# Expert remainders in quarters of 32 slots instead of whole tiles of 128

## The chip, the cores and the metric

The kernel runs on one core of one Trainium2 chip. The metric is the device time of a run in microseconds. The engines are named as the profile names them: PE (TensorE matmul), PEld (its weight load), DVE (VectorE), ACT (ScalarE), POOL (GpSimd) and SP (SyncE, which here issues DMAs).

## The reference

The computation is one gated cross-attention block followed by a mixture of experts, all in float32. There are 8 batches of 256 tokens (2048 tokens, width 256), a context of 120 rows for each batch, 16 heads of 64, and 8 experts with a hidden width of 1024, of which each token uses two.

```python
x = x + tanh(g_xattn[0]) * xattn(layernorm(x), ctx, w_q, w_kv, w_out, b_out)

def ffn(x):                                  # of layernorm(x) again
    probs = softmax(x @ Wr.T)                # 8 experts
    topk_vals, topk_idx = top_k(probs, 2)
    gate = topk_vals / topk_vals.sum(-1)     # placed at the two experts
    h = silu(einsum('btd,efd->btef', x, W1))
    y = einsum('btef,edf->bted', h, W2)
    return einsum('bte,bted->btd', gate, y)

x = x + tanh(g_ffn[0]) * ffn(layernorm(x))
```

The reference computes every expert for every token and weights most of them by zero. The kernel computes only the two chosen experts of each token, so there are 4096 pairs of a token and an expert, here called slots.

## The kernel before, in words

**Attention, 0 to some 272 us.** A loop over 32 units (8 batches, 2 halves of the heads, 2 halves of the tokens) computes projections, scores, softmax and the output projection. Behind it the router picks two experts for each token (`router`), and `places` sends each token's row, with its eight gates and its token number, into a list in memory, `routed`, once for each chosen expert. Each expert has its own stretch of 2048 rows in that list. Rows that no token was sent to stay filled with zeros and a token number past the end, so they add nothing to the output.

**Expert stage, from some 272 us.** The work is done in tiles of 128 slots of one expert. A tile is loaded from the list (`load`), turned so that its 256 columns lie on partitions (`turn`: two PE transposes and a DVE copy), multiplied by W1 (`up`: 16 matmuls of 128 columns and the silu on ACT), multiplied by W2 (`down`: 8 matmuls of 256 columns), scaled by its gates on DVE, and added to its tokens' rows in memory by an indirect add on POOL. The adds wait for one another, one at a time, because two of them may name the same token.

Three kinds of tile follow one another. Eight "first" tiles hold the first 128 slots of each expert; they can start before the router has seen all tokens. Eight "last" tiles hold each expert's last, part-empty 128 slots; their expert is known when the program is built, so their weights are read where they lie, in `w_sb`. The "full" tiles are the whole tiles between; which expert they belong to is known only on the chip, so their place and expert are read from a table (`table`, small DVE operations, built once after tile 4), and DVE first copies the expert's W1 and W2 (2048 elements a partition each, L688 and L697) into fixed buffers. With the full tiles numbered 0 to 28 from the back, 9 to 28 always run, and 0 to 8 are inside a conditional block (L933) that runs only if there are more than 20.

**Order of the work.** PE, DVE, ACT and SP run in the order in which the program is written; POOL's order is the scheduler's. The loop at L930 is software-pipelined: step i does the up of tile i, opens tile i+1 (its weights, its turn), and then does the down of tile i-1. `load` runs four tiles ahead on SP. Up to and including full tile 12 the sums go into a buffer `acc` in memory; then SP copies `acc` to the output (L764) and the last 16 tiles add into the output directly. SP's later loads stand behind that copy in its queue.

Of the kernel before, what the change touches and what calls it, by code (L numbers as in the profile page):

```python
# [33 lines left out]

EARLY = 2
FULLS = 29
SURE = 16
SPARE = 9
# [6 lines left out]
def tile_gated_xattn_moe(  # L45
# [19 lines left out]
    late = ctx.enter_context(tc.tile_pool(name="late", bufs=1))  # L65
# [58 lines left out]
    nc.gpsimd.iota(number, [[P, NBLK]], base=0, channel_multiplier=1)  # L124
    empty = w_sb[:, 2, :XW]
# [453 lines left out]


    def row(tag, n, dtype=F32):
        return small.tile([P, n], dtype, tag=tag, name=tag, bufs=1)

    def table():


        tiles_i = row("tiles_i", E, I32)
        nc.vector.scalar_tensor_tensor(
            tiles_i, count(NBLK, fw[2]), -1.0, bump, ALU.add, ALU.add
        )  # L590
        nc.vector.tensor_scalar(tiles_i, tiles_i, 7, None, ALU.arith_shift_right)
        full = row("full", E)
        nc.vector.tensor_scalar(full, tiles_i, -1.0, 0.0, ALU.add, ALU.max)
        second = row("second", E)
        nc.vector.tensor_scalar(second, first_row, float(P), None, ALU.add)
        last_row = row("last_row", E, I32)
        nc.vector.scalar_tensor_tensor(
            last_row, full, float(P), second, ALU.mult, ALU.add
        )
        upto = row("upto", E)  # L600
        one8 = row("one8", E)
        nc.vector.memset(one8, 1.0)
        nc.vector.tensor_tensor_scan(upto, one8, full, 0.0, ALU.mult, ALU.add)
        total_i = row("total_i", 1, I32)
        nc.vector.tensor_copy(total_i, upto[:, E - 1 : E])

        at = row("at", FULLS)
        nc.gpsimd.iota(
            at, [[1, FULLS]], base=-FULLS, channel_multiplier=0,
            allow_small_or_imprecise_dtypes=True,  # L610
        )
        nc.vector.tensor_scalar(at, at, upto[:, E - 1 : E], None, ALU.add)
        past = fp.tile([P, FULLS, E], F32, tag="y", name="past")
        skipped = fp.tile([P, FULLS, E], F32, tag="y", name="skipped")
        shape = [P, FULLS, E]
        nc.vector.tensor_tensor(
            past,
            upto.unsqueeze(1).to_broadcast(shape),
            at.unsqueeze(2).to_broadcast(shape),
            ALU.is_le,  # L620
        )
        nc.vector.tensor_tensor(
            skipped, past, full.unsqueeze(1).to_broadcast(shape), ALU.mult
        )
        expert = row("expert", FULLS)
        nc.vector.tensor_reduce(expert, past, AX.X, ALU.add)
        expert_i = row("expert_i", FULLS, I32)
        nc.vector.tensor_copy(expert_i, expert)
        before_it = row("before_it", FULLS)
        nc.vector.tensor_reduce(before_it, skipped, AX.X, ALU.add)  # L630
        nc.vector.tensor_tensor(before_it, at, before_it, ALU.subtract)
        nc.vector.tensor_scalar(before_it, before_it, float(P), None, ALU.mult)
        nc.vector.scalar_tensor_tensor(
            expert, expert, float(T), before_it, ALU.mult, ALU.add
        )
        used = row("used", FULLS)
        nc.vector.tensor_scalar(used, at, 0.0, None, ALU.is_ge)
        nc.vector.tensor_scalar(expert, expert, float(P - NOWHERE), None, ALU.add)
        nc.vector.tensor_tensor(expert, expert, used, ALU.mult)
        full_row = row("full_row", FULLS, I32)  # L640
        nc.vector.tensor_scalar(full_row, expert, float(NOWHERE), None, ALU.add)
        return last_row, expert_i, full_row, total_i
# [5 lines left out]
    def take(pool, shape, tag, name, **kw):  # L648
        if spare is None:
            return pool.tile(shape, F32, tag=tag, name=name, **kw)  # L650
        if tag not in spare:
            spare[tag] = pool.tile(shape, F32, tag=tag, name=name, **kw)
        return spare[tag]


    def load(t):
        kind, i = t
        xt = take(fp, [P, XW], "xt", f"xt_{kind}{i}", bufs=6)
        if kind == "first":
            first = nc.sync.dma_start(xt, routed[ds(i * T, P), :])  # L660
            for send in behind:
                tc.declare_no_dep(
                    first.ins, send.ins, reason="rows behind those of the first tiles"
                )
            firsts.append(first)
            return xt
        last_row, _, full_row, _ = tables[0]
        if kind == "last":
            start = nc.sync.value_load(
                last_row[0:1, i : i + 1], min_val=0, max_val=NOWHERE - P  # L670
            )
        else:
            start = nc.sync.value_load(
                full_row[0:1, i : i + 1], min_val=0, max_val=NOWHERE
            )
        nc.sync.dma_start(xt, routed[ds(start, P), :])
        return xt

    def weights(t, xt):

        kind, i = t
        if kind != "full":
            w2 = part(i, DC * DFF, FC, D)
            return part(i, 0, DC, DFF), xt[:, D + i : D + i + 1], lambda: w2
        expert_i = tables[0][1]
        e = nc.vector.value_load(expert_i[0:1, i : i + 1], min_val=0, max_val=E - 1)
        w1 = take(fw[0], [P, DC, DFF], "w1", f"w1_{i}")
        nc.vector.tensor_copy(  # L688
            w1.rearrange("p c f -> p (c f)"),
            w_sb[:, ds(e, 1), : DC * DFF].rearrange("p e f -> p (e f)"),  # L690
        )
        gate = take(fp, [P, 1], "gate", f"gate_{i}", bufs=4)
        nc.vector.tensor_copy(gate, xt[:, D : D + E][:, ds(e, 1)])

        def copy_w2():
            w2 = take(fw[0], [P, FC, D], "w2", f"w2_{i}")
            nc.vector.tensor_copy(  # L697
                w2.rearrange("p c d -> p (c d)"),
                w_sb[:, ds(e, 1), DC * DFF :].rearrange("p e f -> p (e f)"),
            )  # L700
            return w2

        return w1, gate, copy_w2
# [9 lines left out]
    def up(t, xT, w1):  # L713
# [10 lines left out]
        hT = take(fp, [P, FC, P], "hT", f"hT_{t[0]}{t[1]}")  # L724
# [5 lines left out]
    def down(t, hT, gate, xt, w2):  # L730
        py = take(fw[2], [P, 512], "mm", f"py_{t[0]}{t[1]}")
        for f in range(FC):
# [7 lines left out]
        y = take(fp, [P, D], "y", f"y_{t[0]}{t[1]}")  # L740
        nc.vector.tensor_scalar(y, py[:, :D], gate, None, ALU.mult)  # L741
        sure = t[0] == "full" and t[1] >= FULLS - SURE
        add = nc.gpsimd.indirect_dma_start(  # L743
            out=out[:, :] if sure else acc[:, :],
            out_offset=bass.IndirectOffsetOnAxis(
                ap=xt[:, XID : XID + 1].bitcast(I32), axis=0
            ),
            in_=y,
            in_offset=None,
            compute_op=ALU.add,  # L750
        )

        if last_add:
            tc.add_manual_dep(
                add.ins,
                last_add[-1].ins.name,
                mybir.DependencyInfo(
                    mybir.DependencyClass.Sync, mybir.DependencyReason.DATA
                ),
                reason="sums of one token",  # L760
            )
        last_add.append(add)
# [4 lines left out]

    fw = []
    state = {"ready": None, "pending": None}
# [15 lines left out]
    order += [("last", e) for e in range(E)]  # L785
    order += [("full", j) for j in range(SPARE, FULLS)]
    AHEAD = 4
# [130 lines left out]

    for name, kw in (
        ("fw", {}),  # L920
        ("ps_ph", {"space": bass.MemoryType.PSUM}),
        ("ps_py", {"space": bass.MemoryType.PSUM}),
    ):
        fw.append(
            ctx.enter_context(tc.tile_pool(name=name, bufs=2, reuse_waits="tile", **kw))
        )
# [3 lines left out]
    for i, t in enumerate(order):  # L930
        if i == 16:

            with tc.If(total > FULLS - SPARE):  # L933
                spare = {}
                for j in range(SPARE):
# [4 lines left out]
                    down(tj, up(tj, turn(tj, xt), w1), gate, xt, w2)  # L940
                spare = None
        if i == 12:
            total_i = tables[0][3]
            total = nc.values_load(total_i[0:1, 0:1], min_val=0, max_val=FULLS)
        w2_of = state["ready"][2][2]
        if i == 2:
            turn_y(B - 1, bank_tr)
        new = go_up()
        copies = []
# [9 lines left out]
        if i + 1 < len(order):  # L959
            open_tile(order[i + 1], xts[i + 1])  # L960
        if i == 0:
# [9 lines left out]
        state["pending"] = *new, w2  # L971
        if i == 1:
# [10 lines left out]
        if i == 4:  # L983
            tables.append(table())
        while len(xts) <= min(i + AHEAD, len(order) - 1 if tables else 7):
            xts[len(xts)] = load(order[len(xts)])
        if i == 1:
# [46 lines left out]
```

## Time and profile before

| | |
|---|---|
| Time, median of 3 runs | 560.39 us (560.38 to 560.48) |
| The profiled execution's own time | 560.78 us |
| Its span | 559.0 us |
| TensorE clock granted in the span | 0.995 |
| PE busy | 545.2 us, 98% |
| DVE, ACT, POOL busy | 267.5, 192.3, 117.9 us |
| PE idle between 331 and 397 us | 0.0 us |
| PE idle between 397 and 551 us | 2.2 us |

A row of the profile gives the line, the engine, the operation, what is written and read with the shapes, how often, the busy time and the mean duration of one, and then the idle time of the engine just before those instructions with what ended it. Matmuls are pipelined, so the durations of neighbours overlap; the step from one start to the next tells what one costs. The rows in order of time begin with the start and the duration in microseconds.

### The profile page before, as it was taken

To read this page: it belongs to the slowest core of one execution; us is meant where nothing else is said; L and a number is where in the kernel's file an instruction comes from. 1 tells how busy PE (TensorE), PEld (TensorE's weight loads), DVE (VectorE), ACT (ScalarE), POOL (GpSimd) and SP (SyncE) were. 2 spreads that over 40 slices of the span, in tenths; PEclk is the share of its full clock that TensorE was granted. 3 is DMA by queue.
4 is the path that set the end of the run, shared out by engine and by line. 5 is a ranking of instruction groups with operands and counts; after the bars stand their busy time and mean duration, and the time that the engine had idled before them with its cause. 6 is when DMAs were issued, how large, how long until landed. Compare 5 with 4: busy or idle time off the path is not lost. (4 is left out here: it accounts for less than half of the span.)

```text
span 559.0 us, 9985 instructions
## 1 busy us (share of the span) xinstructions
PE 545.2 (98%) x3830; PEld 475.4 (85%) x3830; DVE 267.5 (48%) x612; ACT 192.3 (34%) x669; POOL 117.9 (21%) x129
## 2 busy tenths in 40 slices
PE   8999999999999999999999999999999999999992
PEld 7788878878788787887788999999999999999992
DVE  2666565568665686545743431111344444444430
ACT  1676464664655546556501211111111111111110
POOL 1021100101341013200035442222222132112222
PEclk9999999999999999999999999999999999999998
DMA  8999980500515001120499432222222522222111
GB/s 294 335 315 300 292 225 1 170 21 25 204 41 171 20 21 39 40 59 1 168 351 336 121 88 38 39 31 38 42 38 34 167 55 44 40 38 39 20 20 19
DMA packets 47586, 60.65 MB, mean 108 GB/s; under 512 B 3088, under 2 KB 42640, under 8 KB 47504
## 3 DMA queue, kind: packets, MB, share of 16 engines
q1 hardware_dynamic: 40400, 50.26, 29.3%
q0 software_dynamic: 6720, 9.06, 9.4%
q10 hardware_dynamic: 416, 0.66, 0.4%
q8 instruction: 32, 0.52, 0.4%
q14 instruction: 18, 0.15, 0.1%
HBM read 31.17 MB, written 30.89 MB: 111 GB/s over the span
## 5 line engine op out<-in xcount | busy, mean ns | idle before, releaser
L505 ACT ACTIVATE pr<-psc,mx 128x120 f32<-128x120 f32 x256 | 88.2, 370 | 64.2 <-DVE mx L499 64.2
L717 PEld LDWEIGHTS ph_full<-xT_full,w 128*128 128x128 f32 x640 | 74.5, 192 | 1.6 <-issue 0.7
L717 PE MATMUL ph_full<-xT_full,w 128*128 128x128 f32 x640 | 74.8, 276 | 0.3 <-PEq L933 0.3
L733 PE MATMUL py_full<-w,hT_full 128*128 128x256 f32 x320 | 72.2, 380 | 0.0
L733 PEld LDWEIGHTS py_full<-w,hT_full 128*128 128x128 f32 x320 | 59.4, 190 | 7.2
L725 ACT ACTIVATE hT_full<-ph_full 128x1024 f32<-128x1024 f32 x20 | 20.5, 1024 | 125.0 <-PE ph_full L717 125.0
L455 PE MATMUL pq<-xnT,w_sb 128*128 128x256 f32 x256 | 62.7, 389 | 0.4 <-DVE xnT L174 0.4
L549 PE MATMUL pw<-w_sb 128*128 128x256 f32 x256 | 58.6, 383 | 0.0
L455 PEld LDWEIGHTS pq<-xnT,w_sb 128*128 128x128 f32 x256 | 46.7, 190 | 10.7 <-issue 3.1
L505 ACT ACTIVATION_READ_ACCUMULATOR pr<-psc,mx 128x1 f32 x256 | 55.4, 216 | 0.0
L549 PEld LDWEIGHTS pw<-w_sb 128*128 128x128 f32 x256 | 47.5, 190 | 8.7 <-issue 2.5
L493 DVE TENSOR_REDUCE mx<-psc 128x8 f32<-128x960 f32 x32 | 37.0, 1157 | 37.0 <-PE psc L485 36.8
L743 POOL DMA_INDIRECT out_dram<-y_full,xt_full x16 | 26.5, 1658 | 86.5 <-DVE y_full L741 69.4
L332 POOL DMA_INDIRECT routed<-rows,slot x32 | 31.7, 992 | 56.4 <-DVE slot L328 49.4
L525 ACT COPY w_sb<-tr 120x512 f32<-120x512 f32 x64 | 34.6, 596 | 19.4 <-PE tr L524 19.4
L514 DVE TENSOR_TENSOR pr<-pr,sm 128x960 f32<-128x960 f32 x32 | 37.0, 1158 | 1.1
L485 PE MATMUL psc<-kT,w_sb 64*128 64x120 f32 x512 | 37.2, 284 | 0.0
L485 PEld LDWEIGHTS psc<-kT,w_sb 64*128 64x128 f32 x512 | 31.2, 187 | 6.4 <-issue 3.4
L524 PEld LDWEIGHTS tr<-ident,pr 128*120 128x120 f32 x256 | 29.5, 138 | 5.9 <-issue 4.3
L524 PE MATMUL tr<-ident,pr 128*120 128x128 f32 x256 | 33.5, 273 | 0.1
L440 PEld LDWEIGHTS pk<-ctxT_sb,w_sb 128*128 128x128 f32 x256 | 30.9, 192 | 0.8
L534 PE MATMUL po<-w_sb 120*64 120x256 f32 x256 | 31.3, 386 | 0.0
(138 smaller groups left out, 697.3 us busy)
## 6 DMA issues: line engine op xcount, KB each, us to landing
routed<-w_sb SPq DMA_DIRECT2D x8, 2120.0 KB, 22.3
w_sb<-in_w1T_dram SPq DMA_DIRECT2D x8, 1024.0 KB, 5.4
w_sb<-in_w2T_dram SPq DMA_DIRECT2D x8, 1024.0 KB, 10.3
xt_full<-routed SPq DMA_DIRECT2D x20, 132.5 KB, 2.1
acc<-x SPq DMA_DIRECT2D x8, 256.0 KB, 2.4
x<-in_x_dram SPq DMA_DIRECT2D x7, 256.0 KB, 2.8
w_sb<-in_w_kv_dram SPq DMA_DIRECT2D x3, 512.0 KB, 8.6
xt_first<-routed SPq DMA_DIRECT2D x8, 132.5 KB, 2.9
```

What stands on the lines that cost most here:

```text
L332: send = nc.gpsimd.indirect_dma_start(out=routed[:, :], out_offset=bass.IndirectOffsetOnAxis(ap=slot[:, i : i + 1], axis=0), in_=rows[h][: ...
L455: nc.tensor.matmul(pq[:, i, :], lhsT=wq_sb[:, c, ts(2 * h + i, P)], rhs=xnT[:, c, :], start=(c == 0), stop=(c == DC - 1),)
L485: nc.tensor.matmul(psc[:, j, ts(i, M)], lhsT=qT[ts(j, DH), 4 * o + i, ts(nb, P)], rhs=kT[ts(j, DH), 4 * o + i, :], start=True, stop=True,)
L493: nc.vector.tensor_reduce(mx.rearrange("p (j i) -> p j i", i=4), psc[:, :, : 4 * M].rearrange("p j (i m) -> p j i m", m=M), AX.X, ALU.max,)
L505: nc.scalar.activation(pr[:, h, :], psc[:, j, ts(i, M)], AF.Exp, bias=mx[:, h : h + 1], scale=QK_SCALE, accum_out=sm[:, h : h + 1],)
L514: nc.vector.tensor_tensor(pr, pr, sm.unsqueeze(2).to_broadcast([P, 8, M]), ALU.mult)
L524: nc.tensor.transpose(tr[:M, i, :], pr[:, 4 * j + i, :], ident)
L525: nc.scalar.copy(pT_sb[:, ts(j, 4), ts(nb, P)], tr[:M, :, :])
L534: nc.tensor.matmul(po[ts(j, DH), k, :], lhsT=v_sb[b % 2][:, ts(2 * (4 * o + i) + j, DH)], rhs=pT_sb[:, 4 * j + i, :], start=True, stop=True,)
L549: nc.tensor.matmul(pw[:, :D], lhsT=oT_sb[b % 2][:, ci, ts(k, P)], rhs=wo_sb[:, ci, :], start=(ci == 0), stop=(ci == IC - 1),)
L717: nc.tensor.matmul(ph[:, f, :], lhsT=w1[:, c, ts(f, P)], rhs=xT[:, c, :], start=(c == 0), stop=(c == DC - 1),)
L733: nc.tensor.matmul(py[:, :D], lhsT=hT[:, f, :], rhs=w2[:, f, :], start=(f == 0), stop=(f == FC - 1),)
```

## The change

The eight last tiles go. What remains of each expert behind its whole tiles is handled in one of two ways: a remainder of more than 96 slots is still a whole tile (now one of the full tiles, with its weights copied by DVE), and a smaller one is split into quarters of 32 slots. Four quarters, of any experts, make one tile, a "quad". The full tiles are now numbered 0 to 30 and 8 to 30 always run; two quads always run, and full tiles 0 to 7 and quads 2 to 5 are in the conditional block.

A quad is loaded by an indirect gather on POOL. For each quarter, ACT copies the expert's weights into a shared buffer (`fill`), half of the hidden width at a time. The matmuls of a quarter write 32 partitions, each quarter its own. With a half of the hidden width at a time the steps are: fill W1, turn, up, silu and fill W2, transposes of the hidden rows, down. These twelve steps are put between the steps of four whole tiles, tiles 8 to 11 for the first quad and 12 to 15 for the second, in each tile three of them. Each quad ends with four indirect adds of 32 rows, one for each quarter, because one token may be in two quarters.

The table is built in two parts, after tiles 4 and 5. The copy of `acc` to the output comes after full tile 15 instead of 12.

```diff
-FULLS = 29
-SURE = 16
-SPARE = 9
+QUARTER = 32
+FULLS = 31
+SURE = 15
+SPARE = 8
+QUADS = 6
+MIXED = 2
...
     number = const.tile([P, NBLK], I32, name="number")
     nc.gpsimd.iota(number, [[P, NBLK]], base=0, channel_multiplier=1)
+    places_w = const.tile([P, FULLS], F32, name="places_w")
...
+    nc.vector.tensor_scalar(
+        quarter_i, number[:, 0:1], 5, None, ALU.arith_shift_right
+    )
+    lane = const.tile([P, 1], F32, name="lane")
...
+    for q in range(QUADS):
+        nc.vector.tensor_scalar(
+            places_q[:, q : q + 1], quarter_i, float(4 * q), None, ALU.add
+        )
...
+    def sought(tag, at, upto, count, begin, step):
...
+        past = fw[0].tile(shape, F32, tag="w1", name=f"past_{tag}")
+        nc.vector.tensor_tensor(
+            past,
+            upto.unsqueeze(1).to_broadcast(shape),
+            at.unsqueeze(2).to_broadcast(shape),
+            ALU.is_le,
+        )
...
     def table():
...
+        nc.vector.tensor_scalar(tails, left, float(P - QUARTER), None, ALU.is_gt)
...
+        which, first = sought("w", at, upto, counts, begin, P)
...
+        yield expert_i, full_row
+
+        quarters = row("quarters", E)
+        nc.vector.tensor_scalar(quarters, left, 0.0, None, ALU.is_gt)
+        for k in range(1, 3):
+            nc.vector.scalar_tensor_tensor(
+                quarters, left, float(k * QUARTER), quarters, ALU.is_gt, ALU.add
+            )
...
+        which, first = sought("q", places_q, upto_q, quarters, begin[:, :E], QUARTER)
...
+        nc.vector.tensor_tensor(more_i, more, more_q, ALU.add)
+        yield quad_row, own, experts_i, more_i
...
     def load(t):
...
-        if kind == "last":
-            start = nc.sync.value_load(
-                last_row[0:1, i : i + 1], min_val=0, max_val=NOWHERE - P
-            )
+        if kind == "quad":
+            nc.gpsimd.indirect_dma_start(
+                out=xt,
+                out_offset=None,
+                in_=routed[:, :],
+                in_offset=bass.IndirectOffsetOnAxis(
+                    ap=tables[1][0][:, i : i + 1], axis=0
+                ),
+            )
+            return xt
...
+    def add_up(t, y, xt, parts=1):
...
+        for k in range(parts):
+            own = ts(k, P // parts)
+            add = nc.gpsimd.indirect_dma_start(
+                out=out[:, :] if sure else acc[:, :],
+                out_offset=bass.IndirectOffsetOnAxis(
+                    ap=slots[:, k : k + 1], axis=0
                 ),
+                in_=y[own, :],
+                in_offset=None,
+                compute_op=ALU.add,
+            )
+
+            if last_add:
+                tc.add_manual_dep(
+                    add.ins,
+                    last_add[-1].ins.name,
...
+    def quad(j, xt):
...
+        def fill(down, h):
+            w = take(qp[0], [P, 4, DFF], "part", f"part_{j}_{down}_{h}")
+            for q, e in enumerate(es):
+                slab = w_sb[:, ds(e, 1), ds(down * DC * DFF, DC * DFF)]
+                slab = slab.rearrange("p e (a b) -> p (e a) b", b=D if down else DFF)
+                nc.scalar.copy(
+                    w[:, q, :].rearrange("p (a b) -> p a b", b=D if down else DFF // 2),
+                    slab[:, ts(h, FC // 2), :] if down else slab[:, :, ts(h, DFF // 2)],
+                )
+            return w
+
+        w = fill(0, 0)
...
+        for h in range(2):
+            yield
+            xT = turn(("quad", f"{j}_{h}"), xt)
+            yield
+            pu = take(ps_tr, [P, 512], "tr", f"pu_{j}_{h}")
+            for c in range(DC):
+                for q in range(4):
+                    nc.tensor.matmul(
+                        pu[ts(q, QUARTER), :],
+                        lhsT=xT[:, c, ts(q, QUARTER)],
+                        rhs=w[:, q, ts(c, 512)],
+                        start=(c == 0),
+                        stop=(c == DC - 1),
+                    )
+            yield
+            hq = take(qp[0], [P, 512], "hq", f"hq_{j}_{h}")
+            nc.scalar.activation(hq, pu, AF.Silu)
+            w = fill(1, h)
+            yield
+            tr = take(ps_tr, [P, 512], "tr", f"hqT_{j}_{h}")
+            for f in range(4):
+                nc.tensor.transpose(tr[:, ts(f, P)], hq[:, ts(f, P)], ident)
+            hT = take(qp[0], [P, 512], "hqT", f"hqT_{j}_{h}")
+            nc.vector.tensor_copy(hT, tr)
+            yield
+            py = take(fw[2], [P, 512], "mm", f"py_q{j}_{h}")
+            for f in range(4):
+                for q in range(4):
+                    nc.tensor.matmul(
+                        py[ts(q, QUARTER), :D],
+                        lhsT=hT[:, ds(f * P + q * QUARTER, QUARTER)],
+                        rhs=w[:, q, ts(f, D)],
+                        start=(f == 0),
+                        stop=(f == 3),
+                    )
+            if h == 0:
+                half = take(qp[0], [P, D], "half", f"half_{j}")
+                nc.vector.tensor_scalar(half, py[:, :D], gate, None, ALU.mult)
+            else:
+                nc.vector.scalar_tensor_tensor(
+                    half, py[:, :D], gate, half, ALU.mult, ALU.add
+                )
+                add_up(("quad", j), half, xt, 4)
+            yield
+            if h == 0:
+                w = fill(0, 1)
...
-    order += [("last", e) for e in range(E)]
     order += [("full", j) for j in range(SPARE, FULLS)]
+    always = E + FULLS - SURE - SPARE
...
-        if i == 16:
-            with tc.If(total > FULLS - SPARE):
+        if i == always:
+            with tc.If(more > 0):
...
+        if i == always - 4 * MIXED - 1:
+            quads = [quad(j, xt) for j, xt in enumerate(quad_xts)]
+        mixed = i in range(always - 4 * MIXED, always)
+        if mixed and i % 4 == 0:
+            running = quads[(i - always) // 4 + MIXED]
+        if mixed and i != always - 4 * MIXED:
+            next(running)
         new = go_up()
+        if i == always - 4 * MIXED - 1:
+            next(quads[0])
...
         if i + 1 < len(order):
             open_tile(order[i + 1], xts[i + 1])
+        if mixed:
+            next(running)
...
         close_tile()
         state["pending"] = *new, w2
+        if mixed:
+            next(running)
...
         if i == 4:
-            tables.append(table())
+            parts = table()
+            routing_pool.close()
...
+        if 3 < i < 6:
+            tables.append(next(parts))
...
+        if i == 5:
+            quad_xts = [load(("quad", j)) for j in range(MIXED)]
```

## The prediction

> **What bounds the kernel now.** I read the page's busy shares first, then the stretches of the expert stage, then that stage in order of time.
>
> ```profile
> PE 545.2 (98%) x3830; PEld 475.4 (85%) x3830; DVE 267.5 (48%) x612; ACT 192.3 (34%) x669; POOL 117.9 (21%) x129
> PEclk9999999999999999999999999999999999999998
> L717 PE MATMUL ph_full<-xT_full,w 128*128 128x128 f32 x640 | 74.8, 276 | 0.3 <-PEq L933 0.3
> L733 PE MATMUL py_full<-w,hT_full 128*128 128x256 f32 x320 | 72.2, 380 | 0.0
> ```
>
> TensorE is busy for 98% of the span at full clock. The idle time before its two big expert rows is 0.3 and 0.0 us, so nothing else makes the expert stage wait. The 640 instructions of L717 are 20 tiles of 32: the 20 full tiles that always run.
>
> ```profile
> core 0: us, PE busy (x) PEld busy (x) DVE busy (x) ACT busy (x) POOL busy (x), PEclk, DMA share, GB/s
> 331.00:397.00 66.00, 66.00 (x459) 62.34 (x458) 9.47 (x20) 9.32 (x10) 13.88 (x9) 1.00 0.26 43
> 397.00:551.00 154.00, 151.84 (x1031) 142.20 (x1029) 66.69 (x100) 21.39 (x21) 34.91 (x21) 1.00 0.26 48
> ```
>
> From 331 us on PE has no hole while DVE and ACT are mostly idle. Work moved to those two is free as long as it is in time. A tile less is a tile's PE time less.
>
> ```profile
> 444.31 3.74 PE L717 MATMUL ph_full<-xT_full,w 128*128 128x128 f32 x32
> 447.88 0.38 PE L708 MATMUL xtT_full<-ident,xt_full 128*128 128x128 f32 x2
> 448.10 3.62 PE L733 MATMUL py_full<-w,hT_full 128*128 128x256 f32 x16
> 451.55 3.74 PE L717 MATMUL ph_full<-xT_full,w 128*128 128x128 f32 x32
> ```
>
> Start to start, since matmuls overlap at their ends: up 447.88 - 444.31 = 3.57, turn 0.22, down 3.45, together 7.24 us a tile.
>
> **What is removed.** How many tiles fall away is a matter of the data. I worked the reference's router out for its inputs: the experts get 425, 494, 537, 531, 502, 500, 534 and 573 rows. Behind each first tile of 128 there are 20 whole tiles and remainders of 41, 110, 25, 19, 118, 116, 22 and 61. Three exceed 96 and stay whole tiles, so 23 whole places are needed; tiles 8 to 30 are exactly 23. The other five need 2 + 1 + 1 + 1 + 2 = 7 quarters; two quads hold 8. So the conditional block is not entered, and 36 tiles become 31 tiles and two quads. Removed: 5 x 7.24 = 36.2 us of PE.
>
> **What a quad costs on PE.** No row shows a quad, but the attention stage has its kinds of matmul:
>
> ```profile
> 247.03 1.88 PE L467 MATMUL pv<-w_sb,ctxT_sb 128*120 128x512 f32 x4
> 248.74 1.04 PE L524 MATMUL tr<-ident,pr 128*120 128x128 f32 x8
> 249.71 1.16 PE L485 MATMUL psc<-kT,w_sb 64*128 64x120 f32 x16
> 250.80 1.95 PE L534 MATMUL po<-w_sb 120*64 120x256 f32 x16
> 252.67 2.00 PE L455 MATMUL pq<-xnT,w_sb 128*128 128x256 f32 x8
> ...
> 258.71 0.65 PE L186 MATMUL plT<-xn2T,wr_sb 128*32 128x128 f32 x16
> 259.28 3.08 PE L549 MATMUL pw<-w_sb 128*128 128x256 f32 x13
> ```
>
> Each matmul is two instructions. A wide one of 512 columns takes (248.74 - 247.03)/4 = 0.43 us. A quad's up has per half 8 matmuls of 512 columns, so 16 x 0.43 = 6.84 us in sequence; its down has 16 of 256 columns, 32 x 3.45/16 = 6.90. But the four quarters lie in four groups of 32 output columns, as plT's do. There, 16 instructions of 128 columns took 0.57 us; at the up's pace (3.57/32 = 0.112) they would take 1.79 in sequence and 0.45 four at a time. So the groups overlap, at 3.1 times the pace, with 0.12 us over a perfect four. If that 0.12 is a fixed price of each visit, a quad's half costs 6.84/4 + 0.12 = 1.83 up and 1.85 down; if it grows with the columns, 2.2 each. po, with two groups and twice the columns, took 1.87 against 16 x 0.216/2 = 1.72: again 0.15 over, not double. I take it as fixed.
>
> Here the Trainium skill speaks against the change: "TensorE: Matmul & The Clock Gate", Part 3, "Measured speedup vs the span model", gives four packed tiles at 512 columns 3.07 times the pace, not four. By that figure each visit is 6.87/3.07 = 2.24 us, and the eight visits of both quads cost 8 x 0.40 = 3.2 us more. The row of this kernel decides for the centre, the rule for the range.
>
> Per half come the turn of the token rows again (0.22) and four transposes of the hidden rows (4 x 0.97/8 = 0.48; L524). Sum: 0.22 + 0.48 + 1.83 + 1.85 = 4.38 us, four halves 17.5. Bounds: perfect overlap 16.5, the proportional price 20.5.
>
> **What is hidden, and under what.** ACT gets, per half, two fills of four copies of 1024 elements and a hidden activation. The nearest row is L725, 1.02 us for 1024 elements; a fill is then 4.1, plus some 0.4 for its registers. The fill for the down starts behind the half's up and hq (0.6); PE meanwhile does up, turn, transposes and down of whole tiles, 3.57 + 0.22 + 0.48 + 3.45 = 7.7 us, against 5.1. The fill for the second up has 3.57 + 0.44 + 3.45 = 7.5 against 4.5. Behind the fill on ACT is the whole tile's hT, needed only a tile later. Cover gone: a copy of 2 us instead of 1.1 would make PE wait some 1.3 us at each of seven fills.
>
> DVE copies weights from tile 8 on instead of tile 16 (L688 and L697, 1.23 us each): 2.5 us a tile, under 9.4 us of PE per mixed tile. Queued behind a late copy is the next tile's xT, for which PE waits; the slack is over 2 us.
>
> Table: it is built in two parts behind tiles 4 and 5. Before, its 25 operations ended near 327.3 with a 2.2 us wait for the buffer of y, and PE waited 0.15 us for the xT behind it. Now that wait is gone, while the three-dimensional operations grow from 232 to 496 elements (0.4 to some 0.7 us): part one ends at about 327.5, so 0.2 us; part two (27 operations, 6 us) ends at 334.3, before tile 7's up at 335. A quad's gather on POOL waits for the table and an add, and DVE waits for it (about 1.2 us) ahead of tile 8's weights; up to 1 us if it is late. Start: seven tiny DVE operations now lie between the two halves of the first normalization, on PE's path: 0.03 to 0.14 us each (a memset's step, the gate copy of L693), I take 0.5 in all.
>
> **Where a wait moves.** Each quad adds its rows in four indirect adds that wait for one another; the second quad's stand ahead of tile 15's add, the copy of acc to the output, and on SP ahead of the load of tile 20.
>
> ```profile
> 441.83 0.60 SPq L764 DMA_DIRECT2D out_dram<-acc  x1
> 443.37 28.95 SPq L676 DMA_DIRECT2D xt_full<-routed  x6
> 450.77 1.54 POOL L743 DMA_INDIRECT out_dram<-y_full,xt_full  x1 [11.21 <-DMA out_dram<-acc]
> 455.20 2.15 POOL L743 DMA_INDIRECT out_dram<-y_full,xt_full  x1 [2.88 <-issue]
> ```
>
> One add behind another takes 455.20 - 450.77 = 4.43 us with 128 rows. Of 32 rows none is shown. By this row four take 17.7 us; by the skill's "DMA: Bandwidth & Descriptors", "Anatomy of one DMA", a fixed 2.0 us plus little for the bytes, 8.3. Between these ends I take 3.3 each, 13.2. From the end of the quad's last matmul: adds start at 1.3, tile 15's is done at 1.3 + 13.2 + 3.8 = 18.3, the copy and then the load go out by 19.9, and that load lands 6.2 us later (the longest of L676's, right behind the copy), at 26.1. PE wants it at 0.5 + 3 x 7.24 + 3.57 = 25.8: 0.3 us of waiting. By the 4.43 it is 4.8 us, by the rule nothing. DVE's next late y then waits in the same time.
>
> **Sum.** -36.2 + 17.5 + 0.2 + 0.5 + 0.3 = -17.7 us. The profiled execution took 560.78 us (span 559.0, and 1.8 around it), so 543.1; the median 560.39 lies 0.4 lower, so 542.7. I predict 543.
>
> **Rivals.** (1) The chain of adds: 32 rows cost what 128 do, PE waits 4.8 instead of 0.3 us: 547. For it: each add waits for a whole landing. Against: a quarter of the rows. (2) The groups overlap by the skill's factor: + 3.2, 546; with the proportional price of plT likewise. (3) ACT is late: copies from SBUF at 2 us: seven fills x 1.3 = 9, 552. For it: no ACT row reads SBUF at this size; against: 1024 elements in 1.02 us. (4) On the other side: four groups with 512 different moving columns each do not overlap at all. Then a quad's half is 0.70 + 6.84 + 6.90 = 14.4, four 57.8, and -36.2 + 57.8 + 1.0 = +22.6: 583. It decides from an overlap below 8 x 6.87/(36.2 - 3.8) = 1.7 times; plT's 3.1 with different moving columns speaks against it. (5) The change does not do what it says: the conditional block runs. Eight whole tiles at 12 us or more, one after another, put it over 650; the nearest remainder is 3 rows from a quarter's edge, and the page's 20 tiles agree with my count.
>
> **How the numbers follow.** Forecast 0.60, (1) 0.16, (2) 0.13, (3) 0.06, (4) and (5) together 0.05. All of the first three lie between 540.7 (perfect overlap, no waits: 560.4 - 36.2 + 16.5) and 550 (rivals 1 and 2 together); 540.5 to 551 leaves out little more than (3) to (5), and the unknown terms of table, gather and start are in it. A measurement of this kernel tells about 0.2%, 1.1 us, from no change; every case but (4) and (5) is faster by more: 0.94 faster, 0.01 the same, 0.05 slower.
>
> **What would show it.** The rows of up and down with 992 and 496 instructions (31 tiles) instead of 1152 and 576. The quad's up 16 instructions in 1.8 us from start to start, its down 32 in 1.9; 2.2 each is rival 2, near 7 rival 4. Idle time of PE before the quad's matmuls released by ACT shows rival 3. A hole at tile 20's turn, behind a late copy of acc, shows rival 1; the gap between two of a quad's adds is its price. A hole at tile 6 to 8's up would put the table or the gather on the path. A POOL or ACT share far above these counts would show the block entered, and the prediction wrong.

## The result

The kernel after takes 555.99 us (median of 6 runs, 553.2 to 556.61) where the kernel before takes 560.49 (6 runs on the same chip, 560.38 to 560.82). The ratio is 0.9908, 95% interval 0.9886 to 0.993. That is faster, but by 4.5 us where I forecast 17.5, and it lies outside my range. The profiled execution took 555.92 us with a span of 553.8, so the span is 5.2 shorter than before.

The page of the kernel after, its busy shares, the busy tenths of PE in 40 slices of the span, and the rows of the up and the down:

```profile
PE 529.6 (96%) x3796; PEld 448.8 (81%) x3796; DVE 285.7 (52%) x683; ACT 219.8 (40%) x700; POOL 128.3 (23%) x135
PE   7999999999999999999999999999997959999992
L837 PE MATMUL ph_full<-xT_full,w 128*128 128x128 f32 x736 | 87.0, 276 | 3.2 <-PEq L1153 2.3
L853 PE MATMUL py_full<-w,hT_full 128*128 128x256 f32 x368 | 84.9, 385 | 0.0
```

PE's busy time fell by 15.6 us, so the matmuls did go away. But slices 31 and 33, at about 415 to 429 and 443 to 457 us, are no longer full. The row of the up has the 736 instructions of 23 tiles, and 3.2 us of idle time before them where the kernel before had 0.3. The conditional block was not entered.

First the quad itself, PE in order of time in the kernel after (start, duration, instructions):

```profile
350.45 1.92 PE L944 MATMUL pu<-part,xT_quad 128*32 128x512 f32 x16
352.31 3.84 PE L837 MATMUL ph_full<-xT_full,w 128*128 128x128 f32 x32
355.98 0.38 PE L828 MATMUL xtT_full<-ident,xt_full 128*128 128x128 f32 x2
356.20 0.60 PE L958 MATMUL hqT<-ident,hq 128*128 128x128 f32 x4
356.63 3.62 PE L853 MATMUL py_full<-w,hT_full 128*128 128x256 f32 x16
360.18 1.93 PE L965 MATMUL py_q<-part,hqT 128*32 128x256 f32 x32
362.05 3.84 PE L837 MATMUL ph_full<-xT_full,w 128*128 128x128 f32 x32
```

The quad's up takes 352.31 - 350.45 = 1.86 us, its transposes 0.43, its down 1.87. The whole tiles next to it take 0.1 us more each: up 3.67 instead of 3.57, down 3.55 instead of 3.45. The eight tiles with both quads, 342.89 to 419.83, took 76.94 us; without quads they would take 8 x 7.24 = 57.9, so the two quads cost 19.0.

Then the two places where PE stands still, the end of the second quad and what follows:

```profile
417.96 1.93 PE L965 MATMUL py_q<-part,hqT 128*32 128x256 f32 x32
422.15 2.25 PE L837 MATMUL ph_full<-xT_full,w 128*128 128x128 f32 x18 [2.25 <-PEq L1153]
425.38 1.83 PE L837 MATMUL ph_full<-xT_full,w 128*128 128x128 f32 x14 [0.98 <-issue]
427.04 0.38 PE L828 MATMUL xtT_full<-ident,xt_full 128*128 128x128 f32 x2
...
445.21 3.73 PE L837 MATMUL ph_full<-xT_full,w 128*128 128x128 f32 x32
454.72 0.66 PE L828 MATMUL xtT_full<-ident,xt_full 128*128 128x128 f32 x2 [5.78 <-DMA xt_full<-routed]
455.18 5.44 PE L853 MATMUL py_full<-w,hT_full 128*128 128x256 f32 x16
460.45 1.72 PE L837 MATMUL ph_full<-xT_full,w 128*128 128x128 f32 x14
```

First, tile 16's up should start at 419.83 and be through after 3.57. It is through at 427.04, 3.64 late; the kernel before lost 0.55 at the same block, so 3.1 us are new. The releaser is PE's own sequencer at L1153, the branch around the conditional block. Its record (lengths in ns, start in us), and in the kernel before the rows around the same block with the record of its branch:

```profile
L1153 PEldq COMPARE_BRANCH  x1: 3542/3542/3542, 418.4 to 418.4; - x1
```

```profile
396.84 3.62 PE L733 MATMUL py_last<-w_sb,hT_last 128*128 128x256 f32 x16
400.76 3.81 PE L717 MATMUL ph_full<-xT_full,w 128*128 128x128 f32 x32 [0.30 <-PEq L933]
L933 PEldq COMPARE_BRANCH  x1: 3337/3337/3337, 396.6 to 396.6; - x1
```

Before, the branch begins at 396.6, ahead of the whole down, and is over at 400.0, before that down is through at 400.29: it is hidden altogether. After, it begins at 418.4, half a microsecond into the quad's short down; 1.4 of its 3.5 us are covered and 2.1 show. The up behind it then stops a second time, for 0.98 us after 18 of its 32 matmuls.

Second, tile 20's turn should start at 445.21 + 3.57 = 448.78; it waits for its load until 454.72, 5.94 us. That turn then takes 0.46 instead of 0.22, and the down behind it 460.45 - 455.18 = 5.27 instead of 3.45. The windows of the kernel after show why:

```profile
core 0: us, PE busy (x) PEld busy (x) DVE busy (x) ACT busy (x) POOL busy (x), PEclk, DMA share, GB/s
454.70:458.00 3.30, 3.28 (x9) 2.76 (x10) 1.79 (x3) 0.00 (x0) 2.17 (x1) 0.50 0.10 7
```

The granted clock is 0.50 in the 3.3 us behind the hole (full again from about 458.9): 1.8 us more in the down and 0.2 in the turn, 2.1 in all.

Why the load is late is on POOL, in order of time (an idle time before each, with its releaser):

```profile
418.83 1.54 POOL L879 DMA_INDIRECT acc<-y_full,xt_full  x1 [7.05 <-DVE y_full L861]
423.42 1.32 POOL L879 DMA_INDIRECT acc<-half,slots  x1 [3.04 <-DMA acc<-y_full,xt_full]
426.91 2.17 POOL L879 DMA_INDIRECT acc<-half,slots  x1 [2.18 <-DMA acc<-half,slots]
431.35 1.69 POOL L879 DMA_INDIRECT acc<-half,slots  x1 [2.27 <-DMA acc<-half,slots]
435.40 2.05 POOL L879 DMA_INDIRECT acc<-half,slots  x1 [2.36 <-DVE xT_full L830]
441.19 2.74 POOL L879 DMA_INDIRECT acc<-y_full,xt_full  x1 [3.73 <-DVE y_full L861]
```

and on SP's queue:

```profile
446.08 0.61 SPq L900 DMA_DIRECT2D out_dram<-acc  x1
447.85 11.94 SPq L796 DMA_DIRECT2D xt_full<-routed  x3
```

Four adds of 32 rows take 441.19 - 423.42 = 17.8 us, as much as four of the steps of 4.43 us that the kernel before shows with 128 rows. Tile 15's add follows at 441.19, the copy of acc at 446.08, and only then tile 20's load, at 447.85.

The ledger by the two traces: five tiles -36.2, quads +19.0, branch +3.1, hole +5.9, half clock +2.1, table +0.5 (PE waited 0.62 for DVE at tile 6's up, 0.15 before), start +0.1. Sum -5.5. By the traces the last matmul ends 5.6 us earlier (543.5 instead of 549.1); what follows it takes 0.4 longer, so the spans differ by 5.2 and the profiled times by 4.9.

### The profile page after: what moved, and what is told of

It is laid out like the page before. It is cut to its first block, busy times and chain, and to the rows that moved or that the text cites. A ratio compares the mean times of both kernels' runs of the same rounds, so it can differ in the third digit from the quotient of the medians.

```text
span 553.8 us, 10097 instructions
## 1 busy us (share of the span) xinstructions
PE 529.6 (96%) x3796; PEld 448.8 (81%) x3796; DVE 285.7 (52%) x683; ACT 219.8 (40%) x700; POOL 128.3 (23%) x135
## 5 line engine op out<-in xcount | busy, mean ns | idle before, releaser
L837 PEld LDWEIGHTS ph_full<-xT_full,w 128*128 128x128 f32 x736 | 85.2, 192 | 9.2 <-issue 8.5
L837 PE MATMUL ph_full<-xT_full,w 128*128 128x128 f32 x736 | 87.0, 276 | 3.2 <-PEq L1153 2.3
L853 PE MATMUL py_full<-w,hT_full 128*128 128x256 f32 x368 | 84.9, 385 | 0.0
L853 PEld LDWEIGHTS py_full<-w,hT_full 128*128 128x128 f32 x368 | 69.6, 194 | 8.9
L845 ACT ACTIVATE hT_full<-ph_full 128x1024 f32<-128x1024 f32 x23 | 23.5, 1023 | 108.6 <-PE ph_full L837 108.6
L861 DVE TENSOR_SCALAR y_full<-py_full,gate 128x256 f32<-128x256 f32 x23 | 11.1, 484 | 51.1 <-PE py_full L853 44.7
L926 ACT COPY part<-w_sb 128x1024 f32 x32 | 31.1, 1043 | 14.8 <-PE py_q L965 14.2
```

Of the source, the lines that this page charges most:

```text
L837: nc.tensor.matmul(ph[:, f, :], lhsT=w1[:, c, ts(f, P)], rhs=xT[:, c, :], start=(c == 0), stop=(c == DC - 1),)
L853: nc.tensor.matmul(py[:, :D], lhsT=hT[:, f, :], rhs=w2[:, f, :], start=(f == 0), stop=(f == FC - 1),)
L926: nc.scalar.copy(w[:, q, :].rearrange("p (a b) -> p a b", b=D if down else DFF // 2), slab[:, ts(h, FC // 2), :] if down else slab[:, :, t ...
```

## The experiments

The theory after this: the chain of ordered adds makes the hole, the hole makes the half clock, and the branch is a loss of its own, which lost its cover. The rivals: the small adds are not what is late (the copy or the load itself is); the slow down has another cause; the branch has become dearer in itself. All edits are to the kernel after. The kernel before took 560.51 us beside the first four runs and 560.71 beside the last four.

**Fewer adds in the second quad.**

```diff
-        for k in range(parts):
+        for k in range(1 if t == ("quad", 1) else parts):
```

> The second quad issues only its first indirect add; the sums of its other three quarters are left out of the output. Theory (the chain of adds): three links of some 4.4 us fall out of the chain ahead of tile 15's add, so the copy of acc starts near 433 us instead of 446 and tile 20's load lands near 442, before PE asks for it at 449. The hole of 5.9 us at tile 20's turn and the 1.8 us of half clock behind it go: 556.0 - 8 = 548 us. Rival (the conditional block and its bookkeeping on POOL and SP set the copy's start): no change, 556.

Measured 548.16 us (547.9 to 548.37), ratio 0.9779 (0.9763 to 0.9796). PE in order of time in this run:

```profile
445.41 3.73 PE L837 MATMUL ph_full<-xT_full,w 128*128 128x128 f32 x32
448.99 0.38 PE L828 MATMUL xtT_full<-ident,xt_full 128*128 128x128 f32 x2
```

Tile 20's turn comes right behind the up before it, and there is no slow down. The gap at the branch is still there (2.41 and 1.07 us). So three adds of 32 rows hold the whole hole, with its half clock: 7.8 us.

**The dose: one add less.**

```diff
-        for k in range(parts):
+        for k in range(3 if t == ("quad", 1) else parts):
```

> The second quad issues three of its four adds (its last quarter holds no rows for these inputs, so nothing is missing). If the hole at tile 20's turn is the length of the chain of adds, one add of about 4.4 us less makes it 5.9 - 4.4 = 1.5 us. If the half clock after the hole comes only from a long pause, it is gone too: 556.0 - 4.4 - 1.8 = 549.8. Rival: any pause brings the half clock; then 551.6. Rival: an add of rows that all point outside costs nothing, so that leaving it out changes nothing: 556.

Measured 549.21 us (548.69 to 549.41), ratio 0.9794 (0.9778 to 0.981). PE in order of time in this run:

```profile
449.53 0.41 PE L828 MATMUL xtT_full<-ident,xt_full 128*128 128x128 f32 x2 [0.75 <-DMA xt_full<-routed]
449.77 3.62 PE L853 MATMUL py_full<-w,hT_full 128*128 128x256 f32 x16
```

The hole is 0.9 us (449.53 against 448.61 due) instead of 5.9, and the down behind it takes 3.46. One add less is worth 5.0 us of hole and the half clock behind it, 6.8 by the medians. By the count of seven quarters that add's rows all point outside, and it cost a full one's time; the rival that it is free falls. A pause of 0.75 us brings no half clock.

**Eight rows an add.**

```diff
+            n = P
+            if parts > 1:
+                n, own = 8, ds(k * P // parts, 8)
...
-                    ap=slots[:, k : k + 1], axis=0
+                    ap=slots[:n, k : k + 1], axis=0
```

> Each of the quads' eight adds takes only the first 8 of its quarter's 32 rows, so the sums of the other 24 are left out. If an indirect add has a fixed price whatever its rows, as 32 against 128 rows say, the second quad's four still take about 17.5 us, the hole stays at 5.9 us and the time at 556. Rival: part of the price goes with the rows or with their landing (a third of it, say): four adds 4 x 1 us shorter, hole 2 us, no half clock: 550.

Measured 556.67 us (555.66 to 557.46), ratio 0.9926 (0.991 to 0.9943). The second quad's first add and tile 15's add in this run:

```profile
424.79 1.33 POOL L882 DMA_INDIRECT acc<-half,slots  x1 [3.98 <-DVE gate L813]
...
441.76 2.74 POOL L882 DMA_INDIRECT acc<-y_full,xt_full  x1 [3.69 <-DVE y_full L861]
```

Four adds of 8 rows take 17.0 us; four of 32 took 17.8 in the kernel after and 15.6 to 17.9 in the other runs that have all four. From 32 rows to 8 nothing is saved that shows: nearly all of the price is the add's own, not its rows'.

**Matmuls in the hole.**

```diff
+            if order[i + 1] == ("full", 20):
+                warm = take(ps_tr, [P, DC, P], "tr", "warm")
+                for _ in range(24):
+                    nc.tensor.matmul(
+                        warm[:, 0, :], lhsT=ident, rhs=ident, start=True, stop=True
+                    )
             open_tile(order[i + 1], xts[i + 1])
```

> 24 matmuls whose result is not used are put on PE ahead of tile 20's turn, about 24 x 0.22 = 5.3 us, inside the hole of 5.9 us. If the slow down behind the hole (5.27 us instead of 3.45) comes from the pause of PE, it is back at 3.45 and the time is 556.0 - 1.8 = 554.2, with tile 20's turn no earlier. Rival: the down is slow for what the load or the copy does to the memory at that time, not for the pause: 556.0. If the 24 matmuls end after the load lands, the time is longer by what they overshoot.

Measured 554.6 us (554.31 to 555.7), ratio 0.9893 (0.9876 to 0.9909). PE in order of time in this run:

```profile
449.12 5.52 PE L1196 MATMUL warm<-ident 128*128 128x128 f32 x48
455.68 0.41 PE L828 MATMUL xtT_full<-ident,xt_full 128*128 128x128 f32 x2 [1.04 <-DMA xt_full<-routed]
455.93 3.62 PE L853 MATMUL py_full<-w,hT_full 128*128 128x256 f32 x16
```

The load comes no earlier (the turn is 6.56 us after its due time), but the next up starts at 459.38, so the down is back at 3.45, and the granted clock in these 3.3 us is 1.00. The slow down was the pause of PE. The median gained 1.4 us, not the whole 2.1: in this profile the turn came at 455.68, 0.96 later than in that of the kernel after.

**The copy on POOL's queue.** It still waits for tile 15's add, but tile 20's load no longer stands behind it.

```diff
-            move = nc.sync.dma_start(out, acc[:T, :])
+            move = nc.gpsimd.dma_start(out, acc[:T, :])
```

> The copy of acc to the output is issued from POOL's queue instead of SP's, so no load stands behind its wait. Theory: tile 20's load lands near 443 and the hole at its turn goes (-8 us), but the adds are as late as before, so DVE's y of tile 18 waits for its buffer and tile 21's weights, queued behind it on DVE, come late; some 3 us of PE waiting come back there: 551 us. Rival (the load is slow because of the copy's traffic, whatever queue it is in): 556. Rival (the chain of adds holds nothing but the SP queue): 548.

Measured 550.69 us, ratio 0.9834 (0.9804 to 0.9864). The four runs lie apart: 548.68, 549.14, 552.24, 552.43. In the profiled one (548.68) the load lands in time and tile 20's turn is at 449.13. Its load of tile 20 on SP and its copy on POOL:

```profile
438.33 29.65 SPq L796 DMA_DIRECT2D xt_full<-routed  x5
444.22 0.60 POOL L900 DMA_DIRECT2D out_dram<-acc  x1 [3.58 <-DMA acc<-y_full,xt_full]
```

So it is standing behind the copy in SP's queue that makes the load late. The rival of the copy's traffic is not ruled out as a part of it: here the load goes out 5.9 us before the copy, so it meets neither the queue nor the traffic. Behind the copy it went out at 447.85 and took 6.9 us to land, where such a load took 2.1 in the kernel before (its median); the longer landing alone would be 4.8 us of the hole. In that trace DVE waits 6.67 us for the next add ahead of tile 18's y, and PE for 0.2. Whether that wait reaches PE in the runs of 552 is not shown: they have no trace.

**The branch alone.** The conditional block and the read of its count are taken out.

```diff
-        if i == always:
-            with tc.If(more > 0):
-                spare = {}
...
-        if i == always - 4:
-            more = nc.values_load(tables[1][3][0:1, 0:1], min_val=0, max_val=FULLS)
```

> The conditional block is left out (it is not entered with these inputs, so nothing computed is missing). Theory: the branch's uncovered 2.3 + 1.0 us on PE at tile 16 go, but tile 20's load is late by the chain of adds all the same, so the hole at tile 20's turn grows from 5.9 to some 8 us, and only what POOL saves behind the block (about 1 us) is gained: 554 to 556 us. Rival (the losses add up, the branch costs its own 3.1 us): 552.9.

Measured 553.74 us (553.4 to 555.73), ratio 0.9888 (0.9867 to 0.9909): 2.2 us less. PE in order of time in this run:

```profile
441.71 3.73 PE L837 MATMUL ph_full<-xT_full,w 128*128 128x128 f32 x32
452.88 0.66 PE L828 MATMUL xtT_full<-ident,xt_full 128*128 128x128 f32 x2 [7.44 <-DMA xt_full<-routed]
```

The gap at the block is gone (tile 16's up runs from 419.87 to 423.54), but PE then reaches tile 20 earlier and waits there longer: the turn is due at 445.28 and comes at 452.88, a hole of 7.6 us instead of 5.9. The load's landing sets the end, so PE's gain at the branch is lost again. What the run gained is what the chain gained: the copy went out at 443.80 instead of 446.08. That is a little more than I had allowed.

**No quads.**

```diff
-        mixed = i in range(always - 4 * MIXED, always)
+        mixed = False
...
-        if i == always - 4 * MIXED - 1:
-            next(quads[0])
```

> Leaves both quads' work out (their gathers stay), so the sums of the seven quarters are missing; the five tiles less remain. My ledger of the two traces: -36.2 for five tiles, +0.6 for the table, and no quads, no chain of their adds, no hole. A whole tile's down stands ahead of the conditional block again, so its branch should be covered as in the kernel before: 560.5 - 35.6 = 524.9. Rival: the branch is dearer in itself because the block now holds four quads as well as eight tiles; then its 3.1 us stay and the time is 528.

Measured 524.92 us (524.71 to 525.08), ratio 0.9359 (0.9343 to 0.9375), as expected. The up behind the block in this run:

```profile
401.55 3.81 PE L837 MATMUL ph_full<-xT_full,w 128*128 128x128 f32 x32 [0.30 <-PEq L1153]
```

With a whole tile's down (397.63 to 401.08) queued ahead of the same block, the branch shows 0.3 us again, as before. The branch's record is 3.5 us long here too, under the same block of eight tiles and four quads. It did not become dearer; it lost its cover, the quad's down being only 1.87 us long.

**Both causes away from the path.** The quads stay in tiles 8 to 15; the block moves to a place ahead of tile 20, behind a whole tile's down, and the copy of acc behind tile 19.

```diff
-SURE = 15
+SURE = 11
...
+    start = E
-        if i == always - 4 * MIXED - 1:
+        if i == start - 1:
...
-        mixed = i in range(always - 4 * MIXED, always)
+        mixed = i in range(start, start + 4 * MIXED)
...
-            running = quads[(i - always) // 4 + MIXED]
-        if mixed and i != always - 4 * MIXED:
+            running = quads[(i - start) // 4]
+        if mixed and i != start:
```

> The quads stay between tiles 8 to 15, but the conditional block comes before tile 20 and the copy of acc after tile 19 (SURE = 11). Theory: four more tiles of 7.24 us with one add of some 4.4 us each let the chain catch up, so no load is late (-8 us); and the block now stands behind a whole tile's down of 3.45 us, which covers most of the branch's 3.5 us as in the kernel before (-3 us): 545 us. Rival (the branch is dearer because the block it jumps over is longer): 548. Rival (the chain does not catch up, the hole moves to tile 24): 553.

Measured 544.83 us (544.78 to 545.29), ratio 0.9721 (0.9705 to 0.9737): 11.2 us better than the kernel after, and the fastest here that leaves out no work. The up behind the block in this run:

```profile
449.40 3.81 PE L837 MATMUL ph_full<-xT_full,w 128*128 128x128 f32 x32 [0.32 <-PEq L1154]
```

The branch is covered though it stands at another place. The copy goes out at 465.50, and no load behind it comes late: between tile 8 and the last down PE waits only for those 0.32 us. The quad's four adds take 17.2 us, much as before, but four whole tiles whose adds step by 4.5 to 5.3 us against PE's 7.24 let it catch up before anything waits for the copy. 544.83 - 524.92 = 19.9 us is the price of two quads; 19.0 of it are the visits on PE. Of the last 0.9 the two traces place 0.1 at tile 16's up, 0.6 behind the last matmul and 0.3 outside the span, less 0.2 ahead of tile 8.

## Why the prediction was wrong

**Removed: right.** Five tiles, -36.2; the run without quads gives -35.8 with the table's +0.5 in it. The count of places and quarters held.

**The quad on PE: right in each term, short by 1.5.** Up 1.83 forecast, 1.86 measured; down 1.85 and 1.87; transposes 0.48 and 0.43. The four groups overlap fully with a fixed price: 6.84/1.86 = 3.7 times the pace, not the 3.07 of rival 2 (that row of the page packs rows of the array; here its columns are packed). Missing was what a quad does to its neighbours: 0.1 us on each of fifteen whole ups and downs within the eight tiles, 1.5 us. 17.5 became 19.0.

**Hidden work: right.** ACT's copy takes 1043 ns, and from 320 us on no PE instruction waits for ACT. The table cost 0.5 instead of 0.2, the start 0.1 instead of 0.5.

**"Where a wait moves": the step that failed.** It had the mechanism, in its order, with "0.3 us of waiting"; the measured hole is 5.94. By its terms, from the second quad's last matmul at 419.83:

| | forecast | measured |
|---|---|---|
| the quad's adds start | 1.3 | 3.6 (behind tile 14's add of 418.83) |
| four adds | 13.2 | 17.8 |
| tile 15's add, copy, load issued | 5.4 | 6.7 |
| load lands | 6.2 | 6.9 |
| together | 26.1 | 34.9 |
| PE wants it | 25.8 | 28.95 (later by the branch) |

The largest error is the four adds. I took 3.3 us as a value between the fixed 2.0 of the Trainium skill and the 4.43 of the row for 128 rows. Its page "DMA: Bandwidth & Descriptors" ("Anatomy of one DMA") prices one transfer; what repeats in this chain is an issue of 1.3 us or more, a landing and the wait for it, and no step of the chain, whatever its rows, was under 3.3. The row of the same instruction in the same chain was the better bound. The first quad's adds step by 3.7, 3.6, 3.6 and 4.1 us (14.9), the second's by 3.5, 4.4, 4.1 and 5.8, where the last step has 1.3 us of POOL's semaphore bookkeeping behind the skipped block; that step takes 5.0 to 5.8 us in the five traces with all four adds or three and the block at that place, 3.5 and 3.6 in the two without. So that the four came to 4 x 4.43 is in part chance: a step of 32 rows can be 3.5 us, and the block and longer issues made up the rest. In the run without the block the second quad's four take 16.7. I also let the chain start from rest, though tile 14's add was under way.

This was rival 1, with 4.8 us of hole and 547, and its sign was the one I had named: a hole at tile 20's turn behind a late copy. That its 4.8 lies near the measured 5.94 is in part luck: the chain was 8.8 us longer than forecast, and the branch, which I had at nothing, held PE back by 3.15 of them. It came with two things that no case of mine held.

**The hole's second price.** A pause of 5.9 us costs 2.1 more in the turn and the down behind it, at half clock. The Trainium skill's "TensorE: Matmul & The Clock Gate", Part 1, "The HAM clock gate", says that the clock halves after an idle window of about 3.4 us and comes back after about 3.4 us of steady work; half of that, an estimate of 1.7 us, is the loss. The traces agree for the long holes, with 0.50 for 4.1 us behind that of 5.9 us and for 4.0 behind that of 7.6 (the run without the block), and for the shortest, with full clock after pauses of 0.75 and 1.04. But 3.4 us is not a safe limit. Behind the branch the clock fell to 0.50 for 3.4 us in two runs (matmuls in the hole, copy on POOL's queue), where PE had paused only 2.46 and 2.45 us; in four others pauses of 2.1 to 2.5 us there left it at 1.00. What decides between them is not shown. In the run with the copy on POOL's queue:

```profile
422.27 5.29 PE L837 MATMUL ph_full<-xT_full,w 128*128 128x128 f32 x32 [2.45 <-PEq L1153]
```

A forecast of a hole must ask whether the clock falls behind it.

**The branch.** The profile I quoted had it in plain sight: "0.3 <-PEq L933 0.3". I read the row as nothing to wait for. The record of the branch on PE's sequencer is 3.3 us long in the kernel before and 3.5 in the kernel after; the whole down of 3.45 us hid it all, and the 0.3 is what came behind both. The change puts a quad's down of 1.87 us at that place, and 3.1 us come out, with the second stop in them. I had costed nothing for it and not asked what hid it.

In all: -17.7 + 1.5 (quads) + 5.6 (hole) + 2.1 (clock) + 3.1 (branch) + 0.3 (table) - 0.4 (start) = -5.5. The run without the block shows that these losses aren't a plain sum: as long as the late load sets the end, the branch is paid for inside the hole.

## What to carry to other kernels

A step that is cut into k ordered DMAs costs nearly k full prices, however little is left in each (here 3.3 us or more with 8 or 32 rows, 4.4 or more with 128); look for the last wait behind the chain (here a copy, and the loads queued behind that) and move that to where the chain has caught up. Where a small piece of work takes the place of a large one ahead of a branch, ask what the large one had hidden; a row with 0.3 us of idle time can stand for a branch of 3.3. When two losses lie one behind the other on different engines, take both away together before judging either.

## What the runs showed of the hardware

- An indirect add of 8, 32 or 128 rows, ordered behind another, steps by 3.3 to 4.9 us (8), 3.5 to 5.4 (32) and 4.4 to 5.6 (128), the step at the block left out. Its issue on POOL alone takes 1.3 to 2.7 us.
- A skipped conditional block holds PE's sequencer for 3.3 to 3.8 us (3.8 in the last experiment); matmuls queued ahead of it run on. The DMA packets of the traces point to what it waits for: in all nine traces with the block, one transfer of 16 KB on the instruction queue q8 falls within the branch's record, and the record ends 1.37 to 1.49 us after that transfer does (in the kernel after it runs from 419.46 to 420.54, and the record ends at 421.98).
- The up behind the branch stops again after 18 matmuls, for 0.56 to 1.11 us, in four of the six traces with a quad's down ahead of the block; in the other two it runs at half clock there. The stop ends 1.20 to 1.44 us behind the next such transfer. That both are waits for instructions is read from these times; no run tests it.
- Switching between whole tiles and groups of 32 columns costs the neighbouring whole tile about 0.1 us.
